# Layer 0 of a four-layer image kernel: TensorE and VectorE in source order, the work between attention units placed by unit

## The chip, the cores and the metric

The kernel runs on one core of one Trainium2 chip. The metric is the device time of one launch in microseconds (us). A core has five engines that run side by side and wait for one another on semaphores: PE (TensorE, matmuls; its weight loads are listed as PEld), DVE (VectorE), ACT (ScalarE), POOL (GpSimd) and SP (SyncE, which here issues nearly all DMAs).

## What is computed

The input is a batch of 4 images of 56 x 56 tokens with 256 channels, in float32. Four layers follow one another, each with a group normalisation ahead and a residual sum behind:

```
x = x + L0(gn(x))   # attention of 8 heads over a 7x7 window, zero padded
x = x + L1(gn(x))   # mixing over the 3136 tokens of an image by similarity, LayerNorm, leaky ReLU
x = x + L2(gn(x))   # neighbourhood attention, two dilations, with bias tables
x = x + L3(gn(x))   # shifted 7x7 window attention, with a bias table and a mask
```

The change touches layer 0. Cut to what matters, it is

```
q, k, v = x @ wq.T + bq, x @ wk.T + bk, x @ wv.T + bv
logits = einsum('ndhw,ndkhw->nkhw', q, unfold(k)) * scale   # k runs over 7x7
out = einsum('nkhw,ndkhw->ndhw', softmax(logits, axis=1), unfold(v))
return out @ wo.T + bo
```

Beside it, during layer 0, the kernel prepares for layer 3 the table of biases `rel_bias_table[rel_index]` with its masks (`table_steps`, line 1863 on).

## The kernel before

**Tiles.** Channels lie on the 128 partitions, in two halves. Tokens come in *chunks* of 8 image rows (448 tokens, 7 per image, 28 in all) for the projections, and in *blocks* of 7 rows (392 tokens, 8 per image, 32 in all) for the attention. A block has 4 *units*, column strips of 16, 12, 12 and 16 columns: units 0 and 3 are wide (112 queries), 1 and 2 narrow (84). There are 128 units.

**A projection chunk.** `prepare` (line 1160) normalises a chunk into `xn`: two DVE operations at L939, one copy on ACT, and a load of the chunk after next. `project_rows` returns six steps: `values` twice (matmuls L971, a DVE copy with bias L975 into `v`, a store to DRAM, L979), `keys` twice (matmuls L945, four ACT copies L1190 into the two layouts kE and kI) and `queries` twice (L945, ACT L1199). Each step takes one of two PSUM buffers `ps_m`.

**A unit.** `attend_pairs` (line 1045 on) goes through the units. For each it calls, in the source: `logits` (gather of the values by DMA, L1224; matmuls L1058 into `ps_s`, one buffer for each half; for one half a DVE sum with the mask, L1065, then an exponential on ACT, L1066; for the other half the exponential first, L1068, then a product with the mask on POOL, L1069), then `both` of the unit before (two POOL sums, L1078), then `w["fill"]()`, which is the other work, then `products` of the unit before (matmuls L1087 into `ps_o`, of the values and of a ones matrix) and its `finish` (DVE: reciprocal L1237 or L1232, for tiles on an edge of the image with a sum L1234 ahead; ACT L990, which keeps a check sum; DVE L1239 into `attn`).

**The other work.** `stream` (line 1269) makes for each block one list of steps: some rows of the list of projections (`rows`: the six steps of each chunk, then `prepare` of the next chunk), the *first looks* at chunks of later images (two DVE statistics each, L894, of a chunk that SP loads for it), loads for the next ones, up to three steps of group statistics (`step_stats`), up to three steps of the table, and in the middle the two steps of `project_out` for the block before (matmuls L945 with w_wo, DVE residual sum L1263; the second also has statistics L894 and a store). `spread` cuts the list in four equal parts by number, one part per unit. Of the projections, the list goes `7 * (7 * r + 12) // 8` rows far by block r.

**What sets the order.** Every dependency is tracked from the source, but the order of instructions on an engine is chosen for layer 0 by the framework's scheduler, a list scheduler with priorities from the source order and costs of its own. An engine named in `tc.manual_schedule` keeps the order of the source instead. Before, layer 0 and layer 2 name none, layer 1 names PE, layer 3 names PE, DVE, ACT and POOL. The call is the last of the lines of the change (`run(0, ...)`, line 2093).

**The start.** Ahead of the stream, `layer0` loads the first image and the weights, takes the statistics of image 0, and runs `prepare(0)`, `prepare(1)`, `prepare(2)` and the projections of chunks 0 and 1.

Of the kernel before, what the change touches and what calls it, by code (L numbers as in the profile page):

```python
# [24 lines left out]
FP = mybir.dt.float32  # L25
# [6 lines left out]
NIMG = 4  # L32
# [798 lines left out]
def direct_blocks(ctx: ExitStack, tc: tile.TileContext, d: dict, watch):  # L831
# [272 lines left out]
        products(held)  # L1104
        held["done"]()

    def spread(units, steps):

        n = len(units)
        for i, w in enumerate(units):  # L1110
            mine = steps[i * len(steps) // n:(i + 1) * len(steps) // n]
            w["fill"] = lambda mine=mine: [f() for f in mine]
            yield w

    def lazily(make, i, n):

        made = []
# [8 lines left out]
    def layer0(early, big, pool, brief):  # L1126
# [3 lines left out]
        def load(r, held=xs, tag="x"):  # L1130
            b, g = divmod(r, NCH)
            held[r] = brief.tile([P, CC, CH], FP, tag=tag, name="x0", bufs=3 if tag == "x" else 4)
            nc.sync.dma_start(out=held[r], in_=tokens_of(0, b, g * CH, CH))

        def first_look(r):

            add_stats(0, *divmod(r, NCH), looks.pop(r))
# [36 lines left out]
        def project_rows(r):  # L1174

            b, g = divmod(r, NCH)
            xn = xns.pop(r)
            at = left(g, CH)
            v = brief.tile([P, 4, C], FP, tag="v", name="v0", bufs=1)

            def values(a):
                value_tiles(v, a, g, CH, xn, wv, bv0, vd[b])

            def keys(m):
                pm = project(wk, m * P, lambda h: xn[:, h, at:at + CH], CH)
                rows = pm.rearrange("p (r c) -> p r c", c=S)
                for i in range(NTC):
                    c0, n = key_range(*COLS[i:i + 2])
                    dst = (kE if i in (0, NTC - 1) else kI)[:, m, i // 2, 8 * g:8 * (g + 1), :]
                    nc.scalar.activation(dst, rows[:, :, c0:c0 + n], AF.Identity, bias=bk0[:, m:m + 1])  # L1190

            def queries(m):
                pm = project(wq, m * P, lambda h: xn[:, h, at:at + CH], CH)
                y = 8 * g
                while y < 8 * (g + 1):
                    i, y1 = y // TR, min((y // TR + 1) * TR, 8 * (g + 1))
                    if (b, i) not in q:
                        q[b, i] = brief.tile([P, CC, BT], FP, tag="q", name="q0", bufs=6)
                    nc.scalar.activation(q[b, i][:, m, (y - TR * i) * S:(y1 - TR * i) * S],  # L1199
                                         pm[:, (y - 8 * g) * S:(y1 - 8 * g) * S],  # L1200
                                         AF.Identity, bias=qbias[:, 0, m:m + 1], scale=SCALE)
                    y = y1

            return [lambda f=f, m=m: f(m) for f in (values, keys, queries) for m in range(2)]

        def pair(r, t):

# [48 lines left out]
        def project_out(r):  # L1256
            b, g = divmod(r, NB0)
            x = pool.tile([P, CC, BT], FP, tag="xr", name="xr0")
            nc.sync.dma_start(out=x, in_=tokens_of(0, b, g * BT, BT))

            def step(m):
                pm = project(wo, m * P, lambda h: attns[r][:, h, :], BT)
                nc.vector.scalar_tensor_tensor(x[:, m, :], pm, bo0[:, m:m + 1], x[:, m, :], ALU.add, ALU.add)  # L1263
                if m:
                    add_stats(1, b, g, x)
                    nc.sync.dma_start(out=tokens_of(1, b, g * BT, BT), in_=x)
            return [lambda m=m: step(m) for m in range(CC)]

        def stream():
            n = NIMG * NCH  # L1270
            rows = []
            for c in range(2, n):
                rows += lazily(project_rows, c, 6)
                rows.append(lambda c=c: prepare(c + 1) if c + 1 < n else None)
            look_at = {}
            for b in range(NIMG - 1):
                for i in range(NCH):
                    look_at.setdefault(NB0 * b + min(i // 2 + (b == 0), 3), []).append((b + 1) * NCH + i)
            gone = 0
            for r in range(NIMG * NB0):  # L1280
                b, g = divmod(r, NB0)
                to = min(len(rows), (7 * (7 * r + 12)) // 8)
                steps, gone = rows[gone:to], to
                steps += [lambda i=i: first_look(i) for i in sorted(looks)]
                steps.append(lambda r=r: [load(i, looks, "xs") for i in look_at.get(r + 1, [])])
                for i in range(3 if g > 3 or g == 0 else 0):
                    steps.insert(2 * i, step_stats)
                if r:
                    steps += table[:3]
                    if len(table) in (1, 2, 3):  # L1290
                        steps.append(tables.close)
                    del table[:3]
                    at = (len(steps) + 1) // 2
                    steps[at:at] = project_out(r - 1)
                attns[r] = pool.tile([P, CC, BT], FP, tag="attn", name="attn0")
                yield from spread([pair(r, t) for t in range(NTC)], steps)

        for r in range(3):
            prepare(r)
            if r == 0:  # L1300
                load(3)
            if r < 2:
                for step in project_rows(r):
                    step()
        check_sizes(pool)
        tables = ExitStack()
        both = [tables.enter_context(tc.tile_pool(name=f"t{n}", bufs=n, side="right", reuse_waits="tile")) for n in (1, 2)]
# [555 lines left out]
    def table_steps(big, pool):  # L1863


        NR, NQ = 169, 7
        idx = big.tile([P, WN, WN], I32, name="idx")
        nc.sync.dma_start(out=idx.rearrange("p a b -> p (a b)"), in_=d["relidx"].to_broadcast([P, WN * WN]))
        row = big.tile([P, 2], I32, name="row")
        nc.gpsimd.iota(row, pattern=[[P, 2]], base=0, channel_multiplier=1)  # L1870
        rowf = big.tile([P, 2], FP, name="rowf")
        nc.vector.tensor_copy(rowf, row)
        tab = big.tile([P, 2, NH], FP, name="tab")
        nc.sync.dma_start(out=tab[:, 0], in_=d["table"][:P])
        nc.sync.dma_start(out=tab[:NR - P, 1], in_=d["table"][P:])
        t3 = big.tile([98, 4, 98], FP, name="t3")
        nc.sync.dma_start(out=t3, in_=d["c_m3"])
        base = big.tile([98, NH, WN], FP, name="base")

        def look_up(q0):  # L1880
            idxf = pool.tile([P, NQ, WN], FP, tag="idxf", name="idxf")
            nc.vector.tensor_copy(idxf, idx[:, q0:q0 + NQ, :])
            hot = pool.tile([P, 2, NQ * WN], FP, tag="hot", name="hot")
            for a, n in ((0, P), (1, NR - P)):
                nc.vector.tensor_scalar(hot[:n, a, :], idxf[:n].rearrange("p q k -> p (q k)"),
                                        rowf[:n, a:a + 1], None, ALU.is_equal)
            pb = ps_m()
            for a, n in ((0, P), (1, NR - P)):
                nc.tensor.matmul(pb[:NH, :NQ * WN], lhsT=tab[:n, a, :], rhs=hot[:n, a, :], start=(a == 0), stop=(a == 1))
            tb = pool.tile([NH, NQ, 98], FP, tag="tb", name="tb")  # L1890
            for w in range(2):
                nc.vector.tensor_copy(tb[:, :, w * WN:(w + 1) * WN], pb[:NH, :NQ * WN].rearrange("p (q k) -> p q k", k=WN))
            pt = ps_m()
            for q in range(NQ):
                nc.tensor.transpose(pt[:98, q * NH:(q + 1) * NH], tb[:, q, :], ident[:NH, :NH])
            nc.vector.tensor_copy(base[:, :, q0:q0 + NQ], pt[:98, :NQ * NH].rearrange("p (q h) -> p h q", h=NH))

        def mask(ty):
            m = pool.tile([98, NH, 98], FP, tag="m3", name="m3")
            for w in range(2):  # L1900
                sl = slice(w * WN, (w + 1) * WN)
                nc.vector.tensor_tensor(m[:, :, sl], base, t3[:, ty:ty + 1, sl].to_broadcast([98, NH, WN]), ALU.add)
            mv = m.rearrange("p (q j) k -> p q j k", j=4)[:, :, 2:4]
            nc.scalar.activation(mv, mv, AF.Exp)
            for pair in [3] if ty % 2 else range(3):
                nc.sync.dma_start(out=m3d[:, ty // 2, :, pair, :], in_=m)

        return [lambda q=q: look_up(q) for q in range(0, WN, NQ)] + [lambda ty=ty: mask(ty) for ty in range(4)]

    def check_sizes(pool):  # L1910

# [178 lines left out]
        return tc.tile_pool(name=f"d{l}" + ("e", "", "w", "l")[k], bufs=(2, 1, 2, 2)[k],  # L2090
                            side="right" if l % 2 else "left", reuse_waits="tile")

    run(0, lambda own: layer0(*own), None, range(4))
    with pool_of(2, 0) as early, ExitStack() as ends:
        late = ends.enter_context(pool_of(1, 3))
        held = {}
# [102 lines left out]
```

## Time and profile before

| What | us |
|---|---|
| Median of 3 runs (lowest, highest) | 4027.03 (4025.71, 4041.41) |
| The profiled execution: its own time | 4042.54 |
| Its span, first to last instruction | 4040.7 |
| PE busy in the span | 3848.9 (95%) |
| DVE, ACT, POOL busy in the span | 2356.6, 1381.2, 1746.3 |
| Layer 0's first logits, last residual sum (start) | 38.1, 811.2 |

How to read it: a profile is one execution. Busy time is the union of an engine's instructions; matmuls are pipelined, and a matmul that runs at a lower clock counts as busy for longer. The *granted clock* is the share of full speed that PE was given. Views that are used below: *windows* (busy us of each engine in stretches of the span), *groups* (instructions of one line, engine, operation and shape: count, busy us, mean ns, idle time of the engine ahead of them and what ended it), *waits* (who waited for whom, in total), the *timeline* (instructions in order of time, merged; start, length, engine, line, operation, count, and in brackets the idle time ahead) and the view of a *tile*.

### The profile page before, as it was taken

The page shows a single profiled execution, that of the slowest core. Times are in us where ns is not written, and L with a number is a line of the kernel's source. Part 1 is how long each engine was busy: PE and PEld are TensorE (multiplying, and loading weights), DVE is VectorE, ACT ScalarE, POOL GpSimd, SP SyncE. Part 2 cuts the span into 40 slices and gives each one's busy share as a digit, 9 for nine tenths or more (in the row PEclk, how much of TensorE's full clock was granted, in tenths as well). Part 3 has the DMA queues.
Part 4 walks back from the last instruction along what each step waited for, and adds up shares of the span by engine and source line. Part 5 has one row for each costly group of instructions (what it writes and reads, how often), then busy time and mean ns, then how long its engine had stood idle before and what let it go on. Part 6 is the DMA issues. An engine that isn't in the chain of part 4 may idle for free.

```text
span 4040.7 us, 92344 instructions
## 1 busy us (share of the span) xinstructions
PE 3848.9 (95%) x38871; PEld 2716.9 (67%) x38871; DVE 2356.6 (58%) x4431; ACT 1381.2 (34%) x2927; POOL 1746.3 (43%) x1883
## 2 busy tenths in 40 slices
PE   7999999899999999999999999999999999899998
PEld 4566666566777667776777757776676766566665
DVE  6777777734444434444344443445687887666765
ACT  3444545422222222222222212221555555344443
POOL 3566667721123311233112321124677777555555
PEclk9999999999999999999999999999999999999999
DMA  8443333320000100001000000001344443434443
GB/s 270 108 131 109 111 117 105 96 102 6 19 23 20 40 6 15 24 24 31 6 19 19 29 19 1 19 10 37 105 127 126 124 127 114 151 118 128 134 127 94
DMA packets 268659, 301.84 MB, mean 75 GB/s; under 512 B 25926, under 2 KB 260584, under 8 KB 267752
## 3 DMA queue, kind: packets, MB, share of 16 engines
q1 hardware_dynamic: 267946, 295.76, 23.8%
q8 instruction: 308, 5.05, 0.5%
q14 instruction: 117, 0.96, 0.1%
q10 hardware_dynamic: 288, 0.08, 0.0%
HBM read 203.39 MB, written 92.37 MB: 73 GB/s over the span
## 4 chain that ended last, share of the span: by engine, by line
PE 48%; DVE 4%; POOL 2%; issue 1%; DMA 0%; ACT 0%; POOLq 0%; DVEq 0%; SPq 0%; ACTq 0%
PE ps_m L945 13%; PE ps_o L1492 6%; PE ps_s L1408 6%; PE ps_v L1497 6%; PE ps_m L971 4%; PE ps_o L1087 3%; PE ps_s L1058 3%; PE ps_o L1027 2%; PE ps_t L1478 1%; PE ps_s L1012 1%; DVE rs L1783 1%; PE ps_m L1376 1%; PE ps_m L1363 0%; DVE e L1065 0%; DVE rs L2017 0%
## 5 line engine op out<-in xcount | busy, mean ns | idle before, releaser
L1420 DVE TENSOR_TENSOR acc<-acc,ps_v 128x257 f32<-128x257 f32 x1104 | 455.6, 421 | 686.2 <-PE ps_v L1497 671.5
L1497 PE MATMUL ps_v<-xw,e 128*128 128x257 f32 x2208 | 613.1, 382 | 19.7 <-DVE acc L1420 18.1
L1492 PE MATMUL ps_o<-xw,at 128*128 128x257 f32 x2208 | 609.0, 379 | 0.0
L1408 PE MATMUL ps_s<-xnT,xd 128*128 128x512 f32 (+3 forms) x1344 | 571.1, 547 | 0.0
L1481 ACT COPY at<-ps_t 128x512 f32<-128x512 f32 (+3 forms) x332 | 170.8, 515 | 1050.4 <-PE ps_t L1478 1050.4
L1497 PEld LDWEIGHTS ps_v<-xw,e 128*128 128x128 f32 x2208 | 408.6, 189 | 171.1 <-issue 80.4
L1078 POOL TENSOR_TENSOR b<-e 126x336 f32<-126x336 f32 (+5 forms) x512 | 499.5, 996 | 8.4 <-ACT e L1066 0.3
L1492 PEld LDWEIGHTS ps_o<-xw,at 128*128 128x128 f32 x2208 | 419.1, 190 | 60.1
L945 PE MATMUL ps_m<-xn,w_wqkv 128*128 128x392 f32 x1024 | 383.0, 508 | 5.6 <-DVE vt L975 4.2
L1401 POOL TENSOR_SCALAR xd<-xnT,vec 128x128 f32<-128x128 f32 x192 | 115.0, 611 | 631.9 <-PE ps_s L1408 629.4
L1069 POOL TENSOR_TENSOR e<-e,m0t 126x672 f32<-126x672 f32 (+3 forms) x128 | 238.7, 1865 | 277.2 <-ACT e L1068 264.3
L1069 POOL TENSOR_TENSOR e<-e,bias 119x784 f32<-119x784 f32 (+5 forms) x128 | 244.4, 1910 | 179.4 <-ACT e L1068 178.2
L1408 PEld LDWEIGHTS ps_s<-xnT,xd 128*128 128x128 f32 x1344 | 225.5, 191 | 134.8 <-issue 126.2
L1411 ACT ACTIVATE e<-ps_s 128x512 f32<-128x512 f32 x336 | 185.4, 552 | 335.1 <-PE ps_s L1408 335.1
L990 ACT ACTIVATE no<-rs 128x168 f32<-128x168 f32 (+2 forms) x256 | 93.8, 367 | 597.4 <-DVE rs L1783 273.8
L945 PEld LDWEIGHTS ps_m<-xn,w_wqkv 128*128 128x128 f32 x1024 | 190.4, 193 | 130.5 <-ACT pr L2039 17.9
L1087 PEld LDWEIGHTS ps_o<-e,vp 124*32 124x32 f32 (+3 forms) x8192 | 177.5, 111 | 143.3 <-issue 99.3
L1087 PE MATMUL ps_o<-e,vp 124*32 124x112 f32 (+3 forms) x8192 | 241.3, 254 | 6.2 <-POOL e L1069 4.4
L1066 ACT ACTIVATE e<-e 126x672 f32<-126x672 f32 (+5 forms) x256 | 219.5, 857 | 20.4 <-DVE e L1065 7.7
L939 DVE TENSOR_SCALAR xn<-x,gst 128x28 f32<-128x28 f32 (+4 forms) x368 | 204.5, 609 | 33.1 <-PE ps_m L945 29.0
L1783 DVE RECIPROCAL rs<-ps_o 128x196 f32<-128x196 f32 (+2 forms) x128 | 176.0, 1375 | 80.9 <-PE ps_o L1087 80.0
L1019 POOL TENSOR_TENSOR e<-e,m3l 98x784 f32<-98x784 f32 x64 | 118.3, 1849 | 219.5 <-ACT e L1016 219.5
(196 smaller groups left out, 6337.3 us busy)
## 6 DMA issues: line engine op xcount, KB each, us to landing
x<-xr SPq DMA_DIRECT2D x64, 392.0 KB
x<-in_x SPq DMA_DIRECT2D x53, 448.0 KB
x<-x SPq DMA_DIRECT2D x60, 392.0 KB
xr<-x SPq DMA_DIRECT2D x60, 392.0 KB
vd<-v SPq DMA_DIRECT2D x72, 256.0 KB
xr<-in_x SPq DMA_DIRECT2D x32, 392.0 KB
xr<-x SPq DMA_DIRECT2D x28, 448.0 KB
x<-xr SPq DMA_DIRECT2D x28, 448.0 KB
```

The costliest lines, as they stand in the source:

```text
L939: nc.vector.tensor_scalar(dst, src, gst[:, h, 0:1], gst[:, h, 1:2], ALU.subtract, ALU.mult)
L945: nc.tensor.matmul(pm[:, :n], lhsT=w[:, h, col:col + P], rhs=rhs(h), start=(h == 0), stop=(h == CC - 1))
L1066: nc.scalar.activation(ev, ev, AF.Exp)
L1069: nc.gpsimd.tensor_tensor(parts(ev), parts(ev), w["emask"], ALU.mult)
L1078: nc.gpsimd.tensor_tensor(w["b"][a][:nk, :, :2 * nq].rearrange("p h (i c) -> p h i c", i=2), ev[:, :, :, 0, :], ev[:, :, :, 1, :], ALU.add)
L1087: nc.tensor.matmul(w["o"](k, i)[j * HD:(j + 1) * HD], lhsT=ones[:nk, :HD] if k else v(j, u), rhs=w["b"][j // 2][:nk, j % 2, i * nq:(i + 1) ...
L1408: nc.tensor.matmul(s[:, :n], lhsT=xd[j][:, h, :], rhs=xnT[:, h, first * P:last * P], start=(h == 0), stop=(h == CC - 1))
L1411: nc.scalar.activation(e[:, :n], s[:, :n], AF.Exp, scale=5.0)
L1420: nc.vector.tensor_tensor(acc[:, i, :], acc[:, i, :], pv[:, :C + 1], ALU.add)
L1492: nc.tensor.matmul(out[j][:, :C + 1], lhsT=e[:, col(i)] if i == j else at[:, col(i)], rhs=xw[:, i, :], start=(i == j), stop=(i == NB - 1))
L1497: nc.tensor.matmul(pv[:, :C + 1], lhsT=e[:, col(i)], rhs=xw[:, j, :], start=True, stop=True)
L1783: nc.vector.reciprocal(rs.rearrange("p (t c) -> p t c", t=2), pv[:, :, 1, :])
```

## The change

Five things, all in layer 0:

1. PE and DVE keep the order of the source (`{E.PE, E.DVE}` in place of `None`). ACT, POOL and SP are still ordered by the scheduler.
2. `spread` is gone. Each block has four lists `work[0..3]`, one per unit, with fixed places: statistics first in units 0, 2, 3; then the unit's quarter of the block's projection rows; first looks one per unit from unit 0; loads of later chunks in unit 3; one step of the table in each of units 0, 1, 2; the two steps of `project_out` in units 2 and 3.
3. The six steps of a chunk come as values 0, keys 0, values 1, queries 0, keys 1, queries 1.
4. A table look-up is two steps, `look_up` (compare, matmul, copies) and `turn` (transposes, copy), so that the table has 18 steps for 11.
5. Projections start one chunk further on: chunk 2 and `prepare(3)` are done ahead of the stream, and the 175 remaining rows are spread evenly over 31 blocks, `len(rows) * (r + 1) // (nb - 1)`, but never later than the next block needs them (`needed`).

```diff
-            return [lambda f=f, m=m: f(m) for f in (values, keys, queries) for m in range(2)]
+            return [lambda f=f, m=m: f(m) for f, m in ((values, 0), (keys, 0), (values, 1), (queries, 0), (keys, 1), (queries, 1))]
...
         def stream():
-            n = NIMG * NCH
+            n, nb = NIMG * NCH, NIMG * NB0
             rows = []
-            for c in range(2, n):
+            for c in range(3, n):
                 rows += lazily(project_rows, c, 6)
                 rows.append(lambda c=c: prepare(c + 1) if c + 1 < n else None)
...
+            def needed(r):
+
+                b, g = divmod(min(r + 1, nb - 1), NB0)
+                last = min(TR * (g + 1) + 3, S)
+                c = next(c for c in range(NCH) if c == NCH - 1 or (c + 1) * CH // P * P >= last * S)
+                return max(min(len(rows), len(rows) * (r + 1) // (nb - 1)), 7 * (b * NCH + c - 3) + 6)
+
             gone = 0
-            for r in range(NIMG * NB0):
+            for r in range(nb):
                 b, g = divmod(r, NB0)
-                to = min(len(rows), (7 * (7 * r + 12)) // 8)
-                steps, gone = rows[gone:to], to
-                steps += [lambda i=i: first_look(i) for i in sorted(looks)]
-                steps.append(lambda r=r: [load(i, looks, "xs") for i in look_at.get(r + 1, [])])
-                for i in range(3 if g > 3 or g == 0 else 0):
-                    steps.insert(2 * i, step_stats)
+                to = needed(r)
+                work = [rows[gone + (to - gone) * u // NTC:gone + (to - gone) * (u + 1) // NTC] for u in range(NTC)]
+                gone = to
+                for u, i in enumerate(sorted(looks)):
+                    work[u].append(lambda i=i: first_look(i))
+                work[3].append(lambda r=r: [load(i, looks, "xs") for i in look_at.get(r + 1, [])])
+                for u in (0, 2, 3) if g > 3 or g == 0 else ():
+                    work[u].insert(0, step_stats)
                 if r:
-                    steps += table[:3]
-                    if len(table) in (1, 2, 3):
-                        steps.append(tables.close)
-                    del table[:3]
-                    at = (len(steps) + 1) // 2
-                    steps[at:at] = project_out(r - 1)
+                    for u in range(3):
+                        if table:
+                            work[u].append(table.pop(0))
+                            if not table:
+                                work[u].append(tables.close)
+                    for u, step in zip((2, 3), project_out(r - 1)):
+                        work[u].append(step)
                 attns[r] = pool.tile([P, CC, BT], FP, tag="attn", name="attn0")
-                yield from spread([pair(r, t) for t in range(NTC)], steps)
+                for u in range(NTC):
+                    w = pair(r, u)
+                    w["fill"] = lambda steps=work[u]: [f() for f in steps]
+                    yield w

         for r in range(3):
             prepare(r)
             if r == 0:
                 load(3)
-            if r < 2:
-                for step in project_rows(r):
-                    step()
+            for step in project_rows(r):
+                step()
+        prepare(3)
...
-            tb = pool.tile([NH, NQ, 98], FP, tag="tb", name="tb")
+            tb = held[q0] = pool.tile([NH, NQ, 98], FP, tag="tb", name="tb")
             for w in range(2):
                 nc.vector.tensor_copy(tb[:, :, w * WN:(w + 1) * WN], pb[:NH, :NQ * WN].rearrange("p (q k) -> p q k", k=WN))
+
+        def turn(q0):
+            tb = held.pop(q0)
             pt = ps_m()
             for q in range(NQ):
                 nc.tensor.transpose(pt[:98, q * NH:(q + 1) * NH], tb[:, q, :], ident[:NH, :NH])
...
-        return [lambda q=q: look_up(q) for q in range(0, WN, NQ)] + [lambda ty=ty: mask(ty) for ty in range(4)]
+        return [lambda f=f, q=q: f(q) for q in range(0, WN, NQ) for f in (look_up, turn)] + [lambda ty=ty: mask(ty) for ty in range(4)]
...
-    run(0, lambda own: layer0(*own), None, range(4))
+    run(0, lambda own: layer0(*own), {E.PE, E.DVE}, range(4))
```

More of the change, by code (lines that the diff above doesn't have):

```diff
@@ L1105, in attend_pairs @@
         held["done"]()
[L1107 to L1113, printed above, removed]
     def lazily(make, i, n):
@@ L1878, in table_steps @@
         base = big.tile([98, NH, WN], FP, name="base")
+        held = {}
         def look_up(q0):
```

## The prediction

> **What bounds the kernel now.** I read first the windows view, one stretch per image of layer 0 (its attention runs from 38 to 812 us of the span), with a full stretch of layer 2 beside it, whose loop is the same `attend_pairs`. Columns: length, then busy us of PE, PEld, DVE, ACT, POOL, then granted clock, DMA share, GB/s.
>
> ```profile
> 38.00:263.00 225.00, 197.85 (x2882) 126.80 (x2881) 173.09 (x269) 95.17 (x222) 123.53 (x96) 0.92 0.54 159
> 263.00:451.00 188.00, 174.16 (x2861) 118.21 (x2852) 137.13 (x189) 91.51 (x217) 125.44 (x102) 0.95 0.36 111
> 451.00:639.00 188.00, 174.18 (x2860) 118.35 (x2860) 137.38 (x190) 91.54 (x217) 125.48 (x101) 0.95 0.36 112
> 639.00:812.00 173.00, 154.39 (x2818) 105.39 (x2810) 132.22 (x185) 84.47 (x190) 125.36 (x100) 0.94 0.32 99
> 2900.00:3300.00 400.00, 396.08 (x6967) 279.24 (x6966) 323.58 (x431) 219.11 (x525) 295.16 (x239) 0.99 0.43 124
> ```
>
> Layer 0 is bound by PE with holes: 700.6 us busy of 774, at a clock of 0.92 to 0.95, where layer 2 keeps PE busy 99%. DVE is next, 580 of 774. The first image is the worst: 225 us, with 173 us of DVE, because all first looks at later images and the table stand there.
>
> The timeline of PE gives its prices, from start to start:
>
> ```profile
> 300.74 0.79 PE L1087 MATMUL ps_o<-e,vp 126*32 126x84 f32 x32
> 301.34 0.47 PE L1087 MATMUL ps_o<-b,ones 126*32 126x84 f32 x16
> 301.74 1.13 PE L1058 MATMUL ps_s<-q,kE 32*124 32x112 f32 x32
> 302.81 0.79 PE L1087 MATMUL ps_o<-e,vp 126*32 126x84 f32 x32
> ...
> 305.64 3.27 PE L945 MATMUL ps_m<-xn,w_wk 128*128 128x448 f32 x8
> 308.85 0.97 PE L1087 MATMUL ps_o<-e,vp 124*32 124x112 f32 x32
> 309.64 0.57 PE L1087 MATMUL ps_o<-b,ones 124*32 124x112 f32 x16
> 310.13 1.12 PE L1058 MATMUL ps_s<-q,kI 32*126 32x84 f32 x32
> ```
>
> Logits 1.07; products of a narrow unit (84 columns) 0.60 + 0.40 = 1.0, of a wide one (112) 0.79 + 0.49 = 1.3; a step of keys or queries 3.21 / 2 = 1.6. From the same view: values 2.0 for 8 passes, so 3.4 for a chunk's 14; both steps of the output projection 2.9. A unit is 2.2 us on average, a chunk 3.2 + 3.2 + 3.4 = 9.8.
>
> DVE's prices, from the groups kept apart by form (mean ns stand after the comma):
>
> ```profile
> L1237 DVE RECIPROCAL rs<-rs 128x224 f32<-128x224 f32 x64 | 99.4, 1552 | 2.1
> L1232 DVE RECIPROCAL rs<-ps_o 128x168 f32<-128x168 f32 x48 | 57.6, 1201 | 32.6 <-PE ps_o L1087 32.4
> L939 DVE TENSOR_SCALAR xn<-x,gst 128x448 f32<-128x448 f32 x56 | 51.9, 965 | 20.7 <-PE ps_m L945 17.6 <-POOL gst L923 3.1
> L1065 DVE TENSOR_TENSOR e<-ps_s,m0t 124x896 f32<-124x896 f32 x48 | 51.8, 1080 | 0.4 <-PE ps_s L1058 0.2
> ```
>
> So `finish` of a wide unit is 0.38 + 1.55 + 0.39 = 2.3 us, of a narrow one 1.2 + 0.33 = 1.55; the mask 1.08 or 0.84; `prepare` 2 x 0.97 = 1.95; a first look 2 x 0.61; the residual sum 0.62 a step, its statistics 2 x 0.57; values 0.4 to 0.7 a step.
>
> [...] after 3.65 us without work the 4 passes of L945 took 2.98 us, where 8 took 2.90 at full clock:
>
> ```profile
> 432.58 2.98 PE L945 MATMUL ps_m<-attn,w_wo 128*128 128x392 f32 x4 [3.65 <-DVE attn L1239]
> ```
>
> [...] The tile view of `hot` fits: 376/386/2045 ns for one form of work; I take the group mean, 0.72.
>
> **Part by part.** *Start.* Chunk 2 now goes ahead of the stream: first logits at 38.1 + 9.4 = 47.5 us (chunk 1 took 28.5 to 38.1). Those 9.8 us of PE leave the stream, so this costs nothing by itself. `prepare(3)` goes with it: 1.95 us DVE under chunk 2's matmuls, one copy on ACT, and the load of chunk 5 (448 KB) on SP's queue, ahead of the gathers; without that cover 2 us, once.
>
> *PE's sum.* 128 units x 2.2 = 283; 32 output projections x 2.9 = 93; 25 chunks x 9.8 = 245; table 11.6 + 4.2 = 16; statistics 2: **639 us**. Before: 26 chunks, 649, in a stream of 774, so 125 us are lost now. They are the 73 us idle, and 700.6 - 649 = 52 us of stretched matmuls, of which a clock of 0.94 explains 0.06 x 774 = 46.
>
> *What goes.* PE's waits for `attn` in mid-block (14.8 us in 8 waits between 100 and 780 us), for the mask's read of ps_s (7.7), for group statistics taken in adjacent steps (4.1 + 7.1): the output projection moves to units 2 and 3, a unit after `attn` is done; the statistics stand in units 0, 2, 3. Look-ups of later images no longer crowd into 45 to 114 us.
>
> *What comes.* In source order unit k is, on PE: logits k, fill k, products k-1; on DVE: mask k, fill k, finish k-1. DVE's finish starts when PE starts the next logits, so mask k+1 and all fill of k+1 stand behind 1.55 to 2.3 us of `finish`. I walked the blocks by these prices. One with seven steps (`prepare` alone in unit 0; v0 k0; v1 q0 and output; k1 q1 and output), DVE 0.8 us late at its start: unit 0: DVE finish to 2.35, mask to 3.45, `prepare` to 5.4; PE logits and products to 2.36, then its next logits wait for the mask until 3.5 and the values for `prepare` until 5.45; from there unit 1 ends at 10.25, unit 2 at 16.8, unit 3 at 23.45, DVE again 0.75 late. PE's sum is 8.84 + 9.8 + 2.8 = 21.4, so **2.0 us** are lost. The index arithmetic of the diff (175 steps over 31 blocks, raised by `needed`) gives the rest:
> - Eight such blocks (16, 17, 21, 24, 25, 27 to 29) x 2.0, and three of fewer steps with `prepare` ahead (11, 18, 22) x 3.3: 26 us.
> - Blocks 1, 3, 6, 8, 23 have `prepare` and the next values in one unit: values wait for 1.55 + 1.08 + 1.95 = 4.6 after the unit's start, where PE comes at 1.1: 5 x 3.3 = 16.
> - Blocks 26, 30 and 31 have no projection at all, in spite of the aim: POOL's 4.3 us for a wide unit (2.09 + 2 x 1.16) and 3.5 for a narrow one (1.63 + 2 x 0.91) give 15.6 a block against PE's 11.7: 3 x 4.2 = 13.
> - Seven look-ups: cast, two compares and a matmul in one unit. DVE has finish 2.3, mask 0.84, often a first look 1.23, cast 0.4, compares 1.2 to 1.4: the matmul may start at 6.0, PE is there at 1.07 + 1.6 = 2.7. By unit 2 to 5 us, sum 24. Behind it wait the products and next logits. The second step, `turn`, in the next unit waits for nothing.
> - The other 18 blocks 0.5: 9. Eight groups of statistics, some 2.5 us of small DVE operations each in one unit: 8. First looks that now stand in order, and wait for their loads: 5.
> - Clock: 14 of these waits are longer than 2 us; the 14.8 us for `attn` above came in such ones. A cold stretch of about 6 us at half clock costs 3: 42. The trace of before doesn't show these waits, so the bounds are 0 (none cools) and 14 x 5 = 70; I take the middle because 2-us gaps were sometimes followed by a low clock and sometimes not.
>
> Sum of losses 143. The end, last products to last residual sum, adds 5 us. 47.5 + 639 + 143 + 5 = 834 against 812: **+21 us**. POOL, ACT and SP keep the scheduler's order; their steps move too. ACT's copies of keys (4 x 0.38) and queries, stores of values (256 KB) and loads and stores of the residual (392 KB) on SP go with their steps. I price that at 0: PE waited for a gather 3.5 us in all between 100 and 780. If that cover goes, rival A has the price.
>
> Against its own execution: 4042.54 (span 4040.7 and 1.8 around it) becomes 4064. That execution lies 15.5 above the median; applied to the median, 4027 + 21 = **4048 us**. Half a per cent (20 us) is about what a measurement of this kernel can tell from no change.
>
> **Rivals.** *A, slower: ACT becomes the wait.* Units 3 have three steps on two ps_m buffers; the third needs the keys' four copies. If ACT's order puts the exponential of the masked half first, which waits for DVE's mask at about 3.4, the copies end at 3.4 + 0.95 + 1.5 = 5.9 where PE needs the buffer at 4.1: 1.8 x 25 blocks = 45, so 4093. It decides once the copies end later than 4.1 us into the unit. For it: ACT now waits 217 us for DVE. Against: ACT is half idle.
> *B, faster: DVE keeps up.* Its sum per block (137 / 8 = 17.2) is under PE's 19.9. If the lags are absorbed, as in layer 2 with PE at 99%, the waits ahead of values alone, the 18 blocks, statistics and looks go (26 + 9 + 8 + 5 = 48) and half the clock's loss (21): 21 - 69 = -48, so 3980. Against: layer 2's DVE order is the scheduler's, and its DVE has 19% free.
> *C, same: the waits stay but don't cool PE.* Clock's loss 14 instead of 42: 4020. That the change does nothing is excluded only for the light blocks: its last projections end in block 29.
>
> **Chances.** My forecast 0.45 (own range 4018 to 4078; half above 4047), A 0.16, B 0.26, C 0.13. Slower 0.22 + 0.16 = 0.38; faster 0.26 + 0.01 = 0.27; same 0.35. Cases of both signs hold much, so the range runs from B to A: 3976 to 4095.
>
> **What would show it.** Right: PE waits of 2 to 5 us at L1889's counterpart for the compares, and of 1 us at logits and values after `prepare`; L945 no longer waiting for `attn`; blocks 26, 30, 31 near 16 us; first logits near 47 us; the first image no shorter than 225. Wrong: PE busy over 96% from 263 us on with a clock of 0.98 (B), or PE waiting for ACT's keys (A).

## The result and the profile after

The changed kernel takes 4077.18 us (median of 4 runs, 4070.13 to 4080.78), the kernel before 4030.27 us beside it (4 runs, 4025.71 to 4041.41): a ratio of 1.0114 with a 95% interval of 1.0094 to 1.0134. It is **slower by 1.1%, some 47 us**, where 21 were forecast.

The profiled execution after took 4070.13 us (span 4068.2). In it the first logits start at 47.6 us (38.1 before) and layer 0's last residual sum ends at 845.5, some 34 us later than before (811.8). A second profile of each kernel (the runs a2 and b2 below) gives 855.0 after and 809.4 before, 46 apart. On average layer 0 is 40 us longer. The other 7 us of the medians' difference can't be placed: from layer 0's end to the end of the span the profiles show 3228.9 and 3222.0 before, 3222.7 and 3226.1 after.

The windows view of the kernel after, one stretch for each image of layer 0 and the full stretch of layer 2 (length, then busy us of PE, PEld, DVE, ACT and POOL, granted clock, DMA share, GB/s):

```profile
47.60:284.00 236.40, 194.70 (x2850) 122.95 (x2849) 172.13 (x235) 90.82 (x209) 127.37 (x98) 0.86 0.43 119
284.00:465.30 181.30, 164.84 (x2835) 111.08 (x2829) 141.55 (x202) 89.59 (x210) 125.74 (x100) 0.96 0.42 128
465.30:656.20 190.90, 170.19 (x2848) 112.97 (x2844) 146.27 (x206) 90.94 (x215) 126.13 (x100) 0.98 0.39 117
656.20:845.50 189.30, 161.63 (x2844) 107.03 (x2836) 137.46 (x191) 86.59 (x196) 124.82 (x98) 0.95 0.33 102
2900.00:3300.00 400.00, 393.72 (x6947) 278.10 (x6947) 320.45 (x424) 218.46 (x521) 296.44 (x240) 0.98 0.43 123
```

Image 0 is the worst again: 236 us for 225, its clock 0.86 for 0.92. Image 1 is 7 us shorter (181 for 188), image 2 is 3 us longer, image 3 is 16 longer. PE is busy 691 of 798 us: the holes, in which it is idle, grew from 73 to 107 us.

The waits of PE in layer 0 after (what waited, the releaser, us in total, times, longest) name the holes:

```profile
PE ps_m L971 <- DVE xn L939: 26.7, 23, 3.6
PE ps_m L1897 <- DVE hot L1893: 24.7, 7, 5.9
PE ps_s L1058 <- DVE e L1065: 12.7, 15, 1.3
PE ps_m L945 <- ACT kE L1182: 10.0, 14, 1.7
...
PE ps_m L921 <- DVE dv L917: 4.8, 1, 4.8
PE ps_m L945 <- DVE v L975: 4.3, 5, 1.6
...
PE ps_m L945 <- DVE attn L1231: 3.1, 1, 3.1
```

Values wait for `prepare` (xn), the table's matmul for its compares (hot), the next logits for the mask's read (e): all three for DVE, as the walk had it. The output projection's wait for `attn` is one of 3.1 us. The groups of DVE kept apart by form, those that the prediction shows of before:

```profile
L1229 DVE RECIPROCAL rs<-rs 128x224 f32<-128x224 f32 x64 | 99.4, 1553 | 2.2
...
L939 DVE TENSOR_SCALAR xn<-x,gst 128x448 f32<-128x448 f32 x56 | 66.1, 1222 | 2.5 <-POOL gst L923 2.5
L1224 DVE RECIPROCAL rs<-ps_o 128x168 f32<-128x168 f32 x48 | 57.5, 1197 | 8.9 <-PE ps_o L1087 7.5 <-ACT kE L1182 1.4
L1065 DVE TENSOR_TENSOR e<-ps_s,m0t 124x896 f32<-124x896 f32 x48 | 51.9, 1081 | 0.0
```

Reciprocals and mask take what they took. The normalisation (L939) takes 1222 ns for 965, for the same work; the last section returns to it.

### The profile page after: what moved, and what is told of

It reads as the page before. It is cut to its first block, busy times and chain, and to the rows that moved or that the text cites. A ratio compares the mean times of both kernels' runs of the same rounds, so it can differ in the third digit from the quotient of the medians.

```text
span 4068.2 us, 92346 instructions
## 1 busy us (share of the span) xinstructions
PE 3844.6 (95%) x38871; PEld 2709.1 (67%) x38871; DVE 2377.0 (58%) x4431; ACT 1379.9 (34%) x2927; POOL 1749.4 (43%) x1883
## 4 chain that ended last, share of the span: by engine, by line
PE 47%; DVE 3%; POOL 2%; issue 1%; DMA 0%; ACT 0%; SPq 0%; DVEq 0%; ACTq 0%; POOLq 0%
PE ps_m L945 12%; PE ps_o L1498 6%; PE ps_s L1414 6%; PE ps_v L1503 6%; PE ps_m L971 4%; PE ps_o L1087 3%; PE ps_s L1058 3%; PE ps_o L1027 2%; PE ps_t L1484 1%; PE ps_s L1012 1%; DVE rs L1789 0%; PE ps_m L1382 0%; PE ps_v L1465 0%; PE ps_m L1369 0%; POOL rstd L1546 0%
## 5 line engine op out<-in xcount | busy, mean ns | idle before, releaser
L939 DVE TENSOR_SCALAR xn<-x,gst 128x28 f32<-128x28 f32 (+4 forms) x368 | 219.5, 651 | 12.8 <-PE ps_m L945 9.7
L971 PE MATMUL ps_m<-w_wqkv,xn 128*128 128x256 f32 (+1 forms) x800 | 205.3, 395 | 8.9 <-DVE xr L1824 4.7
```

Source lines behind the costliest of these rows:

```text
L939: nc.vector.tensor_scalar(dst, src, gst[:, h, 0:1], gst[:, h, 1:2], ALU.subtract, ALU.mult)
L971: nc.tensor.matmul(pm[:k, j * C:(j + 1) * C], lhsT=xn[:, h, first:first + k], rhs=w[:, h, :], start=(h == 0), stop=(h == CC - 1))
```

## Experiments

All were timed in three rounds beside the kernel before, whose medians in the four sets were 4032.70, 4030.95, 4031.43 and 4030.41 us. Ratios are to it.

### Is it the source order, or the places of the work?

Theory S: the source order costs. Theory P: the new places of the other work cost. Four kernels: the changed kernel again; it with all orders left to the scheduler; with PE alone in source order; and the kernel before with its old places in source order.

```diff
# a2: no edit
# auto
-    run(0, lambda own: layer0(*own), {E.PE, E.DVE}, range(4))
+    run(0, lambda own: layer0(*own), None, range(4))
# peonly
-    run(0, lambda own: layer0(*own), {E.PE, E.DVE}, range(4))
+    run(0, lambda own: layer0(*own), {E.PE}, range(4))
# oldfixed, in the kernel before
-    run(0, lambda own: layer0(*own), None, range(4))
+    run(0, lambda own: layer0(*own), {E.PE, E.DVE}, range(4))
```

> The changed kernel once more, for a second profile. In the first pair of profiles the spans differ by 27.5 us (4068.2 against 4040.7), while the medians differ by 47. If the rest lies in layer 0, the last residual sum there comes some 10 us later than 845 us in this profile when its time is near 4080; if it lies outside (clock of the later layers), layer 0 ends at 845 again. I expect 4070 to 4081 us and layer 0's end within 4 us of 845.

> The changed kernel with the scheduler's order on PE and DVE again (None in place of PE and DVE); places, look-up in two steps and late projections stay. Theory S (the waits of the source order cost it: look-ups 25 us, values behind prepare 27 us, logits behind the mask 13 us): nearly all comes back, 4025 to 4045. Theory P (the places cost it: chunk 2 ahead of the stream, blocks 26, 30, 31 without projections, whatever the order): 4065 to 4080.

> The changed kernel with PE alone in source order. Theory S: DVE may take compares and prepare ahead of its finish, so the look-up and prepare waits shrink to a half or less: 4040 to 4060. Theory P: as the changed kernel, 4065 to 4080. If PE's order alone makes it as slow or slower (the scheduler's order of DVE does not fit PE's fixed one), over 4075.

> The kernel before with PE and DVE in source order and nothing else of the change. Theory S: slower than the changed kernel, 4095 to 4140, since its output projection follows attn within a unit, its look-ups wait twice in one step and three statistics steps come together. Theory P: near the kernel before, 4025 to 4045.

| Kernel | us | ratio, 95% interval |
|---|---|---|
| a2 (changed kernel again) | 4080.57 | 1.0116, 1.0089 to 1.0142 |
| auto (all by the scheduler) | 4021.39 | 0.9974, 0.9962 to 0.9985 |
| peonly (PE in source order) | 4019.91 | 0.9967, 0.9956 to 0.9979 |
| oldfixed (before, PE and DVE in source order) | 4080.11 | 1.0112, 1.0088 to 1.0137 |

The order costs, and not the places. The new places without DVE's source order are faster than before by 11 us (auto) and 13 us (peonly). The old places in source order lose 47 us. The signs are those of S throughout, but none of its ranges held: auto and peonly came out below theirs (4025 to 4045 and 4040 to 4060), oldfixed below its 4095 to 4140. P's ranges missed by more. In source order the new places cost what the old ones cost. In a2 layer 0 ends at 855.0 and not within 4 us of 845 as expected, and 9.5 of the 12.9 us by which its span is longer lie in layer 0. The changed kernel's two medians lie around 4079 us, from which the steps below are counted.

PE's own source order costs nothing (4019.91 beside 4021.39). By their profiles auto's gain in layer 0 is the clock's: PE sits idle 72 us (before 73), but the time at half clock (a granted clock of 0.50) falls from 99 to 34 us. Of holes over 2 us auto has 7, the kernel before 10.

### DVE's order alone

```diff
-    run(0, lambda own: layer0(*own), {E.PE, E.DVE}, range(4))
+    run(0, lambda own: layer0(*own), {E.DVE}, range(4))
```

> The changed kernel with DVE alone in source order, PE left to the scheduler. Theory D (DVE's source order is the cost, PE's is free): 4060 to 4090, as the changed kernel. Theory B (only both together hurt, since each leaves the other no way round): 4015 to 4040, as with PE alone or with none.

4060.95 us, 1.0075 (1.0049 to 1.0100), at the lower edge of what theory D had. Taking DVE's order away (peonly) gives back 59 us, taking PE's away 18. So PE's order costs only where DVE's is fixed too. In the profile of dveonly PE waits 18.0 us for xn (26.7 with both orders fixed), 15.8 for the compares (24.7) and 14.9 for the mask (12.7). That in a fixed order what waits holds up everything behind it was an assumption of the prediction's walk; no run tests it by itself.

### One repair at a time

Theory W: each named wait costs what the profile shows, and can be taken out by itself. Theory L: DVE's fixed order as such costs; a wait that is removed comes back at the next place. Three repairs, each with PE and DVE in source order: *prep*, `prepare` two steps earlier in the list of rows; *look3*, the matmul of a look-up in a step of its own, a unit after its compares; *late*, `finish` of a unit behind the logits and the mask that follow it in the source, in layer 0 alone.

```diff
# prep
-                rows += lazily(project_rows, c, 6)
+                steps = lazily(project_rows, c, 6)
+                rows += steps[:4]
                 rows.append(lambda c=c: prepare(c + 1) if c + 1 < n else None)
+                rows += steps[4:]
...
-  7 * (b * NCH + c - 3) + 6)
+  7 * (b * NCH + c - 3) + 7)
# look3
+            held[q0] = hot
+
+        def product(q0):
+            hot = held.pop(q0)
...
-  for f in (look_up, turn)]
+  for f in (look_up, product, turn)]
# late, in attend_pairs
             logits(w)
+            if late:
+                done()
...
-                held["done"]()
+                done = held["done"]
+                if not late:
+                    done()
```

> The changed kernel, both engines in source order, with prepare of the next chunk two steps earlier in the chunk's list (after queries 0, ahead of keys 1). Theory W (single waits in source order): PE's waits for xn, 26.7 us in the changed kernel, go, some of the 12.7 us for the mask too, and some 10 us of the clock: 4038 to 4058. Theory L (DVE's load as such is the bound, holes only move): 4065 to 4082.

> The changed kernel, both engines in source order, with the look-up in three steps: compares; matmul and copies in the next unit; transposes in the one after. Theory W: the 24.7 us of PE's waits for the compares go, and of the 65 us at half clock in the first image a half to two thirds, which is 16 to 22 us: 4030 to 4045. Theory L: the first image is bound by 172 us of DVE in 236, so the holes move to values and masks: 4060 to 4080.

> The changed kernel, both engines in source order, with finish of a unit placed after the next logits in layer 0's loop, so that DVE adds the mask of unit k ahead of finish k-2 instead of behind it. Theory W: PE's 12.7 us for the mask go, nothing else: 4062 to 4072. Theory L: no change, 4070 to 4085, since DVE does the same work by the end of the unit.

prep took 4068.90 us (1.0094, 1.0069 to 1.0118), look3 4081.62 (1.0119, 1.0096 to 1.0143), late 4071.98 (1.0090, 1.0065 to 1.0115). Against the changed kernel that is at most 10 us each, and by these intervals none can be told from no gain. It is what theory L had (look3 1.6 us above its range, late where both ranges overlap). The waits of PE in layer 0 show where they went. First late, then prep:

```profile
PE ps_m L971 <- DVE xn L939: 36.4, 29, 5.2
PE ps_m L1903 <- DVE hot L1899: 24.0, 7, 4.5
PE ps_m L945 <- DVE v L975: 6.5, 10, 1.1
...
PE ps_m L945 <- ACT kE L1188: 3.5, 8, 0.5
```

```profile
PE ps_m L1899 <- DVE hot L1895: 29.5, 8, 6.5
PE ps_m L945 <- ACT kE L1182: 24.4, 18, 2.8
PE ps_m L921 <- DVE dv L917: 11.8, 3, 4.8
PE ps_s L1058 <- DVE e L1065: 8.1, 11, 1.3
```

In late the wait for the mask (12.7) is gone, and that for xn rose from 26.7 to 36.4: PE arrives earlier at the values, and `prepare` still stands behind a `finish`. In prep the wait for xn is gone, and that for the keys' copies rose from 10.0 to 24.4. A unit of prep shows the chain that leads there:

```profile
722.04 1.12 PE L1058 MATMUL ps_s<-q,kI 32*126 32x84 f32 x32
...
723.10 1.77 PE L945 MATMUL ps_m<-xn,w_wk 128*128 128x448 f32 x4
...
724.57 0.85 DVE L1065 TENSOR_TENSOR e<-ps_s,m0t 126x672 f32<-126x672 f32 x1
...
725.45 0.76 ACT L1066 ACTIVATE e<-e 126x672 f32<-126x672 f32 x1
...
726.12 0.37 ACT L1182 ACTIVATE kE<-ps_m,vec 128x152 f32<-128x152 f32 x1
```

The mask, behind `finish`, comes 1.4 us after the end of its logits, ACT's exponential behind the mask, and the first copy of the keys behind that, 1.3 us after their matmuls. One place later PE meets the same lateness of DVE. In look3 the waits for the compares fall to 1.1 us, while xn has 34.7 and the mask 17.7.

### The repairs together, and the kernel before again

If L were all, the repairs together would be worth no more. This set also has the kernel before as b2.

> The changed kernel with both single repairs at once: prepare two steps earlier in the list of rows, and the look-up in three steps. PE and DVE in source order. Theory W (each named wait costs what it shows): the waits for xn (26.7) and for the compares (24.7) are both gone and the time falls by 30 to 50 us, to 4030 to 4048. Theory L (DVE's fixed order as such; a wait that is removed comes back at the next row): 4062 to 4082.

> The changed kernel with three repairs at once: prepare two steps earlier, the look-up in three steps, and finish of a unit behind the next unit's logits with their mask (layer 0 only). PE and DVE in source order. Theory W: with the three named orders mended, PE's waits for xn, compares and mask are gone, and the time is within 10 us of the kernel whose DVE is ordered by the scheduler (4020), so 4015 to 4032. Theory L: it stays above 4050; the waits for DVE have other names, or the same at other places.

> Prepare two steps earlier and the look-up in three steps, but PE alone in source order, DVE's order by the scheduler. Theory L: the scheduler had already moved these operations where they are wanted, so no gain over PE alone in source order (4019.9): 4014 to 4026. Theory W: the source's places still matter as priorities, and 5 to 15 us are gained: 4005 to 4014.

> The kernel before, once more, for a second profile. If the profiled execution before (span 4040.7, layer 0's end at 811.8) was an unlucky one, this one has a span of 4025 to 4032 and layer 0 ends some 10 us earlier, near 800. If the profile is always longer than the median, it is again near 4040 with layer 0's end near 812.

| Kernel | us | ratio, 95% interval |
|---|---|---|
| preplook (prep, look3) | 4070.18 | 1.0101, 1.0084 to 1.0118 |
| all3 (prep, look3, late) | 4027.72 | 0.9989, 0.9980 to 0.9999 |
| preplookpe (prep, look3; PE alone in source order) | 4028.43 | 0.9990, 0.9981 to 0.9998 |
| b2 (before) | 4032.17 | 1.0003, 0.9991 to 1.0014 |

**Theory L falls**: DVE keeps its source order in all3, and 51 of the 59 us are gone. W falls too: all3 lies in its range, but preplook gives 9 us and not 30 to 50. (preplookpe lies 2 us above the higher of its two ranges; a later set comes back to it. In b2 layer 0 ends at 809.4, not near 800 as expected.) A third theory, M: `finish` ahead of the mask and `prepare` ahead of its values delay the same units, so that either one alone keeps PE waiting. It names the pair that counts:

> The changed kernel with two of the three repairs: prepare two steps earlier and finish behind the next logits; look-up in two steps as in the change. The three together gave 4027.7, each alone 4069 to 4082. Theory M (DVE's late finish and the late prepare bind the same units, so only both together free PE): 4030 to 4045, with the waits for the compares (some 25) still there. Theory N (any repair that leaves one of the three is worth little): 4058 to 4075.

> The changed kernel with the other two: look-up in three steps and finish behind the next logits; prepare where the change has it. Theory M: the waits for xn (some 30) stay, 4055 to 4075. Theory N: also 4058 to 4075. If instead finish and the look-up are what counts, 4030 to 4045.

lateprep (prep and late) took 4036.42 us (1.0011, 0.9999 to 1.0022); latelook (look3 and late) 4057.13 (1.0061, 1.0041 to 1.0081). So **M holds**: prep and late, worth 10 and 7 us alone, are worth 43 together. The third repair adds 9. The pair isn't alone in this: late and look3 are worth 22 together, 7 and nothing alone, though PE still waits 45.4 us for xn there; prep and look3 give 9. The scheduler orders ACT, POOL and SP anew in each of these kernels; what that adds wasn't separated. PE's waits in layer 0 of lateprep:

```profile
PE ps_m L1905 <- DVE hot L1901: 26.8, 7, 6.5
PE ps_m L921 <- DVE dv L917: 12.1, 3, 4.8
PE ps_m L945 <- ACT kE L1188: 11.3, 14, 1.6
...
PE ps_m L945 <- DVE v L975: 2.7, 3, 1.3
```

The wait for xn is gone, that for the mask is 0.3 us, and they haven't come back elsewhere: the keys' copies have 11.3, values 2.7. The table's compares stay, as they should: look3 isn't in it.

One unit shows DVE's lateness: block 27, unit 1, in the timeline of the changed kernel, from a narrow unit's logits (726.9) to the next (733.1), with what DVE does just ahead:

```profile
724.40 1.08 DVE L1065 TENSOR_TENSOR e<-ps_s,m0t 124x896 f32<-124x896 f32 x1
...
725.39 3.38 DVE L939 TENSOR_SCALAR xn<-x,gst 128x448 f32<-128x448 f32 x2
...
726.89 1.12 PE L1058 MATMUL ps_s<-q,kI 32*126 32x84 f32 x32
...
728.70 0.38 DVE L1226 TENSOR_TENSOR rs<-ps_o,outside 128x224 f32<-128x224 f32 x1
...
728.83 1.56 PE L971 MATMUL ps_m<-w_wv,xn 128*128 128x256 f32 x6 [0.19 <-DVE xn L939]
729.11 1.55 DVE L1229 RECIPROCAL rs<-rs 128x224 f32<-128x224 f32 x1
...
731.01 0.85 DVE L1065 TENSOR_TENSOR e<-ps_s,m0t 126x672 f32<-126x672 f32 x1
...
733.12 0.68 PE L1058 MATMUL ps_s<-q,kI 32*126 32x84 f32 x16
```

The logits are issued at 726.9, but DVE is still at `prepare` from unit 0 (to 728.8), then at `finish` (to 731.1), and reads the logits for the mask at 731.0, 3 us after their end at 728.0. The same unit of lateprep, where `prepare` has gone to another unit and `finish` stands behind the mask:

```profile
690.44 1.12 PE L1058 MATMUL ps_s<-q,kI 32*126 32x84 f32 x32
...
691.67 0.86 DVE L1065 TENSOR_TENSOR e<-ps_s,m0t 126x672 f32<-126x672 f32 x1 [0.71 <-PE ps_s L1058]
...
692.44 0.38 DVE L1232 TENSOR_TENSOR rs<-ps_o,outside 128x224 f32<-128x224 f32 x1
...
692.86 1.55 DVE L1235 RECIPROCAL rs<-rs 128x224 f32<-128x224 f32 x1
...
695.35 1.12 PE L1058 MATMUL ps_s<-q,kI 32*126 32x84 f32 x32
```

The mask is read 1.2 us after the logits begin, for 4.1, and DVE waits for PE. The lengths of the two units can't be compared: the first has eight passes of values, the second four. The whole block has the same 360 matmuls in both, at full clock. In the windows view, the changed kernel and then lateprep:

```profile
722.57:746.83 24.26, 22.41 (x360) 14.43 (x356) 17.27 (x22) 11.94 (x29) 19.31 (x15) 1.00 0.30 96
686.20:707.80 21.60, 21.08 (x360) 14.24 (x356) 16.68 (x25) 12.56 (x30) 18.71 (x15) 1.00 0.35 110
```

The block takes 21.6 us for 24.3. PE is idle 0.5 us in it for 1.9, and its busy time too is shorter, 21.1 us for 22.4.

### Do the repairs help where the scheduler orders DVE?

> The three repairs with PE alone in source order. If the scheduler's order of DVE already does what the repairs do, 4018 to 4030, as PE alone in source order without them (4019.9) and with two of them (4028.4). If the repairs help it too, 4005 to 4016.

> Finish behind the next logits, PE alone in source order, nothing else. The same two cases: 4018 to 4030 if the scheduler already places DVE's finish well, 4005 to 4016 if the order in the source helps as a priority.

With PE alone in source order all three repairs give 4027.52 us (0.9986, 0.9976 to 0.9996), late alone 4019.08 (0.9967, 0.9957 to 0.9976), none 4019.91 (0.9967). They add nothing there. The two kernels with prep and look3 in them, this one and preplookpe (4028.43), are even some 8 us slower than those without; why is open. **The fastest versions** are peonly and latepe, which can't be told apart: 0.33% under the kernel before, by intervals that exclude no change.

## Why the prediction was right in its sign and too small

**First logits**: forecast 47.5, measured 47.6 (49.4 in a2). Right.

**The holes**: the forecast had 101 us of waits and 5 for the end; measured 105.9 up to the last residual sum (107.1 in a2). Most names fit, too. `prepare` ahead of values 26 + 16 = 42, against 26.7 for xn and 12.7 for the mask, 39.4 together. Look-ups 24 against 24.7; `turn`'s matmuls don't appear. The blocks with no projection 15.6 us each, against 15.4 for blocks 26 and 30. A seven-step block without statistics was walked at 23.45 with 2.0 us lost; blocks 24, 25, 27 and 29 take 24.5, 26.4, 24.3 and 24.7, with PE idle for 3.7, 2.6, 1.9 and 2.2. The image that should be no shorter than 225 us took 236.

That the sum meets the forecast within 1 us is partly luck. ACT's copies of keys, priced at 0, took 10.0 us: rival A's mechanism exists at a quarter of its price. In block 27 the copies end at 744.3, 4.9 us into unit 3, and PE waits 0.6 for them. On the other side no wait for a first look (5) appears, "the other 18 blocks" are 13 beside the 19 named, and 15.6 less 11.7 is 3.9 us a block, not 4.2. The total of the forecast, 834.5, is 22.7 above 811.8 and not 21.

**The step that failed is PE's sum**, the 639 us of matmuls, and with it the balance of PE's busy time. To measure it, take PE's busy time and subtract half of what PE was busy at half clock: there a matmul took twice as long (values 427 ns for 216 at full clock, the output projection 654 for 329). The windows view over all stretches at half clock in layer 0, the sums of before, after and a2 (length, then busy us of each engine):

```profile
sum 99.01, PE 90.55 PEld 55.65 DVE 57.06 ACT 31.14 POOL 45.87; mean PE 6.47 PEld 3.97 DVE 4.08 ACT 2.22 POOL 3.28
sum 102.37, PE 83.64 PEld 49.70 DVE 58.79 ACT 16.18 POOL 45.22; mean PE 5.23 PEld 3.11 DVE 3.67 ACT 1.01 POOL 2.83
sum 109.22, PE 96.49 PEld 58.97 DVE 57.63 ACT 15.78 POOL 37.03; mean PE 5.36 PEld 3.28 DVE 3.20 ACT 0.88 POOL 2.06
```

With these, layer 0 up to the start of its last residual sum divides so:

| us | Before, as the prediction had it | Profile of before | of b2 | Forecast | Profile of after | of a2 |
|---|---|---|---|---|---|---|
| To the first logits | 38.1 | 38.1 | 38.5 | 47.5 | 47.6 | 49.4 |
| Matmuls at full clock | 649 | 654.4 | 655.3 | 639 | 649.5 | 649.6 |
| Lost at half clock | 52 | 45.3 | 41.0 | 42 | 41.8 | 48.2 |
| Holes, the end's 5 us with them | 73 | 73.4 | 73.9 | 106 | 105.9 | 107.1 |
| Sum | 812 | 811.2 | 808.7 | 834.5 | 844.8 | 854.3 |

The sum is 10.5 us short, in both profiles of the changed kernel. Half of it could be seen ahead: of the 52 us of stretched matmuls before, the prediction's own reading of the clock explained 46. The other 6 had no name; they were work that 649 didn't hold, and they were left out of 639 again. The other half comes with the change. Chunk 2 ahead of the stream should have taken 9.8 us out of it, but the sum fell by 5 to 6. A likely reason is that the prices were read from matmuls that follow one another without a break: PE's work is broken off 110 times in layer 0 after, 79 times before and 67 times in lateprep, whose 11358 matmuls, the same as after, take 643.7 us. Block 27 above shows the same. No run changes the breaks alone.

**The clock** was priced at 42 and cost 41.8 in one profile and 48.2 in the other, a right size with some luck: 16 and 18 stretches at half clock (102.4 and 109.2 us in all) for 14, but PE was idle in part of them. The prediction took a stretch as about 6 us; in the profile of before it is 7.1 on average (99.0 us in 14). In the changed kernel a stretch begins during or within 4 us after ten of the 12 holes over 2 us, some of them only 2.2 to 2.7 us long. Of the holes of 1 to 2 us it is 6 of 22, in the kernel before 7 of 14, in auto none of 13: the length of one hole doesn't settle it. What the forecast missed is the balance. Going from 52 to 42, it let a kernel with nearly half more idle time lose less to the clock than before. By the averages of two profiles the loss was 43 before and 45 after. So PE's busy time, forecast to fall by 20 us (700.6 to 681), fell by 3, and this is where the forecast's missing time in layer 0 lies.

**Applied to the median**: 21 of layer 0 became 40 on average over two profiles each. The long base (15.5 above the median) had little part in it: layer 0 ended at 811.8 in that profile and at 809.4 in b2, whose span is 9.3 us shorter. Most of what made it long stood behind layer 0.

**Rivals.** B, DVE keeps up, failed for the reason that the walk gave, DVE's place and not its sum: with the places mended (all3) the same operations in source order cost nothing. Even then the time is 4027.7 and not 3980. C, waits that don't cool PE, is out: it had 14 us lost to the clock, and 42 and 48 were.

## What to carry to other kernels

When an engine that isn't the bottleneck gets a fixed order, look in its queue for long operations that stand ahead of what the bottleneck engine waits for: here `finish` ahead of the mask, and `prepare` just ahead of its values. Mend all such places of one unit together before judging any, since one alone may only move the wait (prep and late: 10 and 7 us alone, 43 together). And let a sum of prices close on the kernel before, down to the last few microseconds, before it is used for the kernel after: time without a name there, 6 us here, is missing again in the forecast.

## What the runs showed of the hardware that was not expected

**The time of DVE's normalisation goes with what POOL does at that moment.** The tile view of `xn` over images 2 and 3 (minimum, median and longest ns; first and last start), the changed kernel and then lateprep:

```profile
L939 DVE TENSOR_SCALAR xn<-x,gst x24: 499/1558/2281, 468.7 to 778.1; 128x448 f32<-128x448 f32 x24
```

```profile
L939 DVE TENSOR_SCALAR xn<-x,gst x26: 441/616/1317, 465.9 to 791.0; 128x448 f32<-128x448 f32 x22, 128x512 f32<-128x512 f32 x4
```

The mean of 965 ns that the prediction used mixes two kinds. Of the normalisations of 448 tokens behind the first logits (50 before, 48 in the others), those with less than half of their time beside a POOL instruction take 0.5 us: 13 before, 2 after, 12 in lateprep. Those over 80% beside one have a median of 1.32 us before (31 of them), 1.98 after (30) and 1.01 in lateprep (29). Of those between, five of six before and all 16 after take 0.5 us too. The windows view of lateprep, images 0 to 3, shows the sum:

```profile
47.70:277.20 229.50, 191.00 (x2850) 121.44 (x2849) 155.26 (x235) 92.34 (x209) 126.23 (x98) 0.88 0.43 123
277.20:452.80 175.60, 162.36 (x2836) 109.17 (x2832) 137.91 (x204) 92.18 (x211) 125.30 (x100) 0.98 0.45 135
452.80:628.40 175.60, 165.88 (x2852) 112.48 (x2848) 136.51 (x206) 93.54 (x215) 124.85 (x100) 0.99 0.41 125
628.40:797.60 169.20, 154.65 (x2840) 104.69 (x2836) 127.33 (x189) 89.37 (x195) 123.38 (x98) 0.98 0.37 113
```

In image 2 the same number of DVE instructions (206) is busy 136.5 us for 146.3, over all four images 557 for 597. No run here moves POOL's work alone, so why the two go together isn't shown. How much of lateprep's gain is this and how much the order itself wasn't separated.

**A gain in layer 0 shows only in part in the whole.** auto, peonly and latepe end layer 0 at 785.2, 783.2 and 789.8 us, 21 to 27 earlier than the mean of before, but their medians are only 11 to 13 us lower. Half clock in layer 1 took 65 to 75 us in their profiles, 61 and 72 in those of before, so one profile each can't say whether something is given back there. In part the profiles were of executions shorter than the median: auto's took 4014.12 us and peonly's 4010.84, 7 and 9 under their medians, but latepe's 4025.57 is 6 over. It stays open.
